# Tile-by-tile pool waits, an early start of the local attention's q and k, and a full-matrix variance in a post-LN decoder

## The chip, the core and the metric

The kernel runs on one NeuronCore of one Trainium2 chip, in float32. Its engines work side by side, each on its own in-order stream: TensorE (PE, with its weight loads shown as PEld), VectorE (DVE), ScalarE (ACT), GpSimd (POOL), and SyncE (SP), which here only starts DMAs. Matmuls write PSUM; DVE and ACT read it; POOL works on SBUF. The metric is the time of one execution on the device in microseconds, lower is better. Before the change it is 2500.81 us, the median of three runs (2500.76 to 2501.01).

## What is computed

Eight sequences of 256 tokens with 128 features pass three sublayers, each followed by a LayerNorm without gain and bias. Cut to what matters:

```python
# x: [8, 256, 128], ctx: [8, 256, 128]
x = layernorm(x + ssm(x))            # LN, conv over 4 tokens, SiLU, selective scan with 16 states, gate
x = layernorm(x + xattn(x, ctx))     # LN of x and of ctx; 16 heads of 64; scores clipped to +-11
x = layernorm(x + ffn(x))            # six layers, below

def ffn(x):
    for d in range(6):
        t = shift_tokens(x)                        # second half of the features from the token before
        q, k, v = split(t @ Wqkv[d], 3)            # 16 heads of 64
        q, k = rotary(l2norm(q) * qs[d]), rotary(l2norm(k) * ks[d])
        x = x + local_attention(q, k, v) @ Wo[d]   # window 32, looks at its own and the previous window
        h = LN(shift_tokens(x)) @ W1[d] + b1[d]
        x = x + (h_a * gelu(h_g)) @ W2[d] + b2[d]
    return x
```

## The kernel before

The features lie on the 128 partitions. Two sequences form a pair of 512 tokens (`TP`), and there are four pairs (`NPAIR`). Three stages follow one another.

**Stage 1** (to L494) runs the state-space sublayer pair by pair: `pre` (a LayerNorm, convolution, projections), `scan` (16 states by 2 halves) and `post` (the closing LayerNorm). Generators of the next and the last pair are advanced step by step inside `scan`. The first pair of stage 2's projections (`project(0)`) runs beside the last scan.

**Stage 2** (L497 to L573) is the cross attention. For each pair it runs 16 items (batch, pair of heads): `weights` (L504) makes scores on PE (L514), clips them on DVE (L520), takes Exp on ACT and adds two halves on POOL (L523); two items later `values` (L526) multiplies by v and sums on PE (L533, L539), takes the reciprocal by Ln and Exp on ACT, and divides on DVE (L546). Beside it `project(p + 1)` (L184) makes q, k and v of the next pair: two LayerNorms and twelve projections, one step per item. For the last pair (p = 3) nothing runs beside. Then come the output projection y2 (L566), the residual r (L570) and the pair's LayerNorm. q, k and v of even pairs lie in a pool on the right side of SBUF (`s2a`), those of odd pairs in the stage's own pool (`s2`), which also holds the items' tiles. `early2.close()` (L573) frees `s2w` (the weights) and `s2a`.

**Stage 3** (L576 to L951) is the six-layer transformer. Its pools `s3c`, `s3w` and `s3` are opened after stage 2's are closed. It clears the padded key tile `kz` (POOL, L589) and three padded value tiles `vz` (DVE, L592), loads rotary tables, mask and the weights of layer 0, and then works through 48 units `seq` of (layer, batch). A list `slots` (L902) gives the hand-made order of the steps in one round `run(n)` (L925): the attention of unit n, with q, k and v of units n + 1 and n + 2 in between, and the feed-forward of the last finished pair as a generator in the "ff" slots. The steps named below are `shift` (copies the shifted tokens, L653 to L655), `query_key` (one projection of 128 tokens to 1024 columns, L663; Square L675 on ACT; two multiplications with the rotary table, L682 and L683, and a sum of squares, L687, on DVE; two additions, L686, on POOL), `root` (a max on DVE, L695; Ln and Exp on ACT), `normalise` (POOL, L706), `turn` (transposes, L713), `value`, `scores` (L760) and `turn_weights` (L791). The rounds begin at n = −2, so that the first two rounds only fill the pipeline. PE's order in stage 3 is exactly the program's (`manual_schedule`, L941); the order on the other engines, and that of stages 1 and 2, is chosen by a scheduler. Four LayerNorms (L950) and the transposing store (L157) end the kernel.

**LayerNorm** (`layernorm_steps`, L101) works on [128 features, 512 tokens]. The mean comes from a matmul with a full matrix of 1/128 (L104), which leaves the mean on every partition; DVE subtracts (L108), ACT squares (L110). The variance comes from four matmuls with one column (L115), so it lies with tokens on partitions as 128x4; ACT takes Ln and Exp of that (L89), and four matmuls with the identity (L128) spread it over all partitions again; DVE multiplies (L135 or L137). `yield`s split it into steps for whoever advances it; with `fine` they lie before other steps than without.

**Pools.** A pool of tiles that is opened where an older one lay waits, at the first use of any of its tiles, for all the older pool's work (`reuse_waits="pool"`, the default). PSUM has one pool for stages 2 and 3 (`ps`, L498) and another for stage 1 (`ps1`), with two buffers for each of the tags "big", "s" and "o".

Of the kernel before, what the change touches and what calls it, by code (L numbers as in the profile page):

```python
# [49 lines left out]
def decoder_kernel(ctx: ExitStack, tc: tile.TileContext, a: dict, out: bass.AP):  # L50
# [8 lines left out]
    def psum(name):  # L59
        return tc.tile_pool(name=name, bufs=2, space=bass.MemoryType.PSUM)  # L60
# [40 lines left out]
    def layernorm_steps(x, dst, g=None, b=None, view=lambda t: t, fine=False):  # L101

        mu = ps_s("ln_mu")
        T.matmul(mu, lhsT=mean_w, rhs=x, start=True, stop=True)  # L104
        if fine:
            yield
        xc = lnp.tile([P, TP], FP, name="ln_xc")
        V.tensor_tensor(xc, x, mu, ALU.subtract)  # L108
        sq = lnp.tile([P, TP], FP, name="ln_sq")
        A.activation(sq, xc, AF.Square)  # L110
        if not fine:
            yield
        var = ps_s("ln_var")
        for j in range(4):
            T.matmul(  # L115
                var[:, j : j + 1], lhsT=sq[:, j * P : (j + 1) * P], rhs=mean_w[:, 0:1],
                start=True, stop=True,
            )
        if fine:
            yield  # L120
        rs = lnp.tile([P, 4], FP, name="ln_rs")
        inv_root(rs, var[:, 0:4], eps_t)
        if not fine:
            yield

        bc = ps_s("ln_bc")
        for j in range(4):
            T.matmul(  # L128
                bc[:, j * P : (j + 1) * P], lhsT=rs[:, j : j + 1].to_broadcast([P, P]), rhs=ident,
                start=True, stop=True,  # L130
            )
        if fine:
            yield
        if g is None:
            V.tensor_tensor(dst, xc, bc, ALU.mult)  # L135
        else:
            V.scalar_tensor_tensor(dst, view(xc), g, view(bc), ALU.mult, ALU.mult)  # L137
            V.tensor_scalar(dst, dst, b, None, ALU.add)
# [33 lines left out]
    pools2 = [early2.enter_context(tc.tile_pool(name="s2a", bufs=1, side="right"))]  # L172
# [325 lines left out]
    banks.append(ctx.enter_context(psum("ps")))  # L498
    with tc.tile_pool(name="s2", bufs=2) as sp:
# [51 lines left out]
        for p in range(NPAIR):  # L551
            cur, nxt = nxt, {}
            ahead = project(p + 1, nxt) if p + 1 < NPAIR else iter(())
# [15 lines left out]
            r = sp.tile([P, TP], FP, name="r2")  # L569
            V.scalar_tensor_tensor(r, y_ps, col("bo"), x1[p], ALU.add, ALU.add)  # L570
            x2[p] = new_x(p)
            layernorm(r, x2[p])
# [3 lines left out]
    with ExitStack() as st:  # L576
        cp = st.enter_context(tc.tile_pool(name="s3c", bufs=1))
        wp = st.enter_context(tc.tile_pool(name="s3w", bufs=2))
        sp = st.enter_context(tc.tile_pool(name="s3", bufs=2))

        rot = cp.tile([P, 4, 2, HD], FP, name="rot")
        nc.sync.dma_start(out=rot, in_=a["c_rot"])
        mask = cp.tile([P, NW, 2 * W], FP, name="mask")
        nc.sync.dma_start(out=mask, in_=a["c_mask"])


        kzs = [cp.tile([P, NHB, 2, W + S], FP, name=f"kz{i}") for i in range(1)]
        for t in kzs:
            G.memset(t, 0.0)  # L589
        vzs = [cp.tile([P, 4, 4, 2, HD], FP, name=f"vz{i}") for i in range(3)]  # L590
        for t in vzs:
            V.memset(t, 0.0)  # L592

        x3 = [new_x(p) for p in range(NPAIR)]
        wts, thirds, tabs = {}, {}, {}

        def load_third(d, c):

            w = wp.tile([P, INNER], FP, name="wqkv", bufs=4)
            nc.sync.dma_start(out=w, in_=a["L0_ffn_Wqkv"][d][:, c * INNER : (c + 1) * INNER])  # L600
            thirds[d, c] = w

        def load_table3(d):
            sc = wp.tile([P, 2, HD], FP, name="sc", bufs=1)
            for i, src in enumerate((a["L0_ffn_q_scale"], a["L0_ffn_k_scale"])):
                nc.sync.dma_start(out=sc[:, i, :], in_=src[d : d + 1, :].to_broadcast([P, HD]))

            tab = wp.tile([P, 4, 2, HD], FP, name="tab")
            for i in range(2):
                V.tensor_tensor(  # L610
                    tab[:, 2 * i], rot[:, 2 * i],
                    sc[:, i].unsqueeze(1).to_broadcast([P, 2, HD]), ALU.mult,
                )
                for u in range(2):
                    o, f = slice(u * 32, u * 32 + 32), slice(32 - u * 32, 64 - u * 32)
                    V.tensor_tensor(
                        tab[:, 2 * i + 1, :, f], rot[:, 2 * i + 1, :, o],
                        sc[:, i, f].unsqueeze(1).to_broadcast([P, 2, 32]), ALU.mult,
                    )
            tabs[d] = tab  # L620

        def load(d):
            wo = wp.tile([P, NHB, D], FP, name="wo3")
            nc.sync.dma_start(out=wo, in_=a["L0_ffn_Wo"][d].rearrange("(k p) e -> p k e", p=P))
            w1 = wp.tile([P, 2 * DFF], FP, name="w1")
            nc.sync.dma_start(out=w1, in_=a["L0_ffn_W1"][d])
            w2 = wp.tile([P, 3, D], FP, name="w2")
            nc.sync.dma_start(
                out=w2[:, 0:2, :], in_=a["L0_ffn_W2"][d][0:256].rearrange("(k p) e -> p k e", p=P)
            )  # L630
            nc.sync.dma_start(out=w2[: DFF - 256, 2, :], in_=a["L0_ffn_W2"][d][256:DFF])
            wts[d] = wo, w1, w2

        def batch(xs, b):
            return xs[b // 2][:, (b % 2) * S : (b % 2 + 1) * S]

        seq = [(d, b) for d in range(DEPTH) for b in range(B)]
        todo = [(wh, g) for wh in range(2) for g in range(2)]

        got = [{} for _ in seq]  # L640

        def shift(n):

            d, b = seq[n]
            if d + 1 < DEPTH:
                if b == 3:
                    load(d + 1)
                    load_table3(d + 1)
                if b == 6:
                    load_third(d + 1, 0)  # L650
            x = batch(x2 if d == 0 else x3, b)
            xs = sp.tile([P, S], FP, name="xs", bufs=3)
            G.memset(xs[HD:, 0:1], 0.0)  # L653
            A.copy(xs[:HD, :], x[:HD, :])
            A.copy(xs[HD:, 1:], x[HD:, : S - 1])  # L655
            got[n]["xs"] = xs
            got[n]["ss"] = sp.tile([P, 4, H], FP, name="ss", bufs=3)
            got[n]["rn"] = sp.tile([P, 4, H], FP, name="rn", bufs=3)

        def proj(n, c, tb, name):  # L660
            pr = ps_big(name)
            for i in range(2):
                T.matmul(  # L663
                    pr[:, i * 512 : (i + 1) * 512], lhsT=got[n]["xs"][:, tb * P : (tb + 1) * P],
                    rhs=thirds[seq[n][0], c][:, i * 512 : (i + 1) * 512], start=True, stop=True,
                )
            return pr

        def query_key(n, c, tb):

            d, b = seq[n]
            pr = proj(n, c, tb, "qk_ps")
            p3 = pr.rearrange("p (h d) -> p h d", h=H)
            sq = sp.tile([P, H, HD], FP, name="sq", bufs=1)
            A.activation(sq, p3, AF.Square)  # L675
            t = sp.tile([P, H, HD], FP, name="qk", bufs=4)
            rb = sp.tile([P, H, HD], FP, name="rb", bufs=1)
            cs, sn = (
                tabs[d][:, 2 * c + k, tb, :].unsqueeze(1).to_broadcast([P, H, HD])
                for k in range(2)  # L680
            )
            V.tensor_tensor(t, p3, cs, ALU.mult)  # L682
            V.tensor_tensor(rb, p3, sn, ALU.mult)  # L683
            for u in range(2):
                o, f = slice(u * 32, u * 32 + 32), slice(32 - u * 32, 64 - u * 32)
                G.tensor_tensor(t[:, :, o], t[:, :, o], rb[:, :, f], ALU.add)  # L686
            V.tensor_reduce(got[n]["ss"][:, 2 * c + tb, :], sq, AX.X, ALU.add)  # L687
            got[n][c, tb] = t
            if tb == 1 and b == B - 1 and d + 1 < DEPTH:
                load_third(d + 1, c + 1)  # L690

        def root(n, c, tb):

            ss, rn = (got[n][x][:, 2 * c + tb, :] for x in ("ss", "rn"))
            V.tensor_scalar(ss, ss, 1e-24, None, ALU.max)  # L695
            inv_root(rn, ss)

        def value(n, tb):
            t = sp.tile([P, INNER], FP, name="v3", bufs=4)
            A.copy(t, proj(n, 2, tb, "v_ps"))  # L700
            got[n]["v", tb] = t

        def normalise(n, c, tb):
            t = got[n][c, tb]
# [111 lines left out]
        def turn_output(n, t):  # L816
            wh, g = todo[t]
            if g == 0:
                got[n]["oT", wh] = sp.tile([P, NHB, P], FP, name="oT3")
# [218 lines left out]
```

## Time and profile before

The profiled execution took 2499.94 us; its span, from the first to the last instruction recorded, is 2498.2 us. Stretches of it, by the first instruction of each:

| stretch | from, us | first instruction |
|---|---|---|
| stage 1 | 0 | |
| stage 2, pair 0 | 383.1 | scores L514 |
| pair 3, alone | about 624 | scores L514 |
| y2 of pair 3 | 677.46 to 683.74 | L566 |
| stage 3, first projection | 693.32 | L663 |
| rounds with attention (n = 0) | 737.73 | L791 |
| closing LayerNorms and store | 2462.55 | L104 |

In the profile, a group of instructions is written as line, engine, operation, names of what is written and read, shapes, and their number; then busy time and mean duration, and how long the engine stood idle before them and on what. A timeline row begins with its start and duration in us. "PEclk" is the clock that TensorE was granted, in tenths of full speed; elsewhere it is given as a fraction.

The share of busy time by engine is PE 92%, DVE 72%, ACT 59%, POOL 57%. The chain of work that ended last, followed back from the end, lies 43% on PE, 32% on DVE, 14% on ACT and 4% on POOL.

### The profile page before, as it was taken

What the parts mean: (1) busy time and instruction counts of PE and PEld (TensorE: products, weight loads), DVE (VectorE), ACT (ScalarE), POOL (GpSimd) and SP (SyncE); (2) the same over time, 40 slices, a digit from 0 to 9 for tenths busy, and PEclk for the clock granted to TensorE, in tenths of its full rate; (3) what the DMA queues carried; (4) which work ended last, traced back from release to release, by engine and by line L of the source; (5) the groups of instructions that cost most, each with busy time, mean ns of one, the idle gap of its engine ahead of it and who ended that gap; (6) DMA issues with size and microseconds to landing.
All of it is one profiled execution on the core that took longest, in us unless ns stands there. A gap on an engine that the chain in (4) does not pass through costs nothing.

```text
span 2498.2 us, 54483 instructions
## 1 busy us (share of the span) xinstructions
PE 2310.4 (92%) x21378; PEld 1456.9 (58%) x21378; DVE 1795.9 (72%) x2661; ACT 1462.7 (59%) x2400; POOL 1432.0 (57%) x1180
## 2 busy tenths in 40 slices
PE   7688789999879999999999999999999999999996
PEld 3233235554446666666666666666666666666664
DVE  4788874444477777777777778777777877777762
ACT  4444444444446666666666666666666666666652
POOL 3889882222367665665656656666655666656630
PEclk9898899999979999999999999999999999999997
DMA  4444430000032223222222223222232223222220
GB/s 125 96 112 108 100 76 5 5 1 1 1 111 65 56 64 72 68 62 59 71 65 69 60 56 82 65 66 56 64 73 62 68 54 75 56 56 56 58 56 17
DMA packets 437963, 154.62 MB, mean 62 GB/s; under 512 B 401295, under 2 KB 417549, under 8 KB 437581
## 3 DMA queue, kind: packets, MB, share of 16 engines
q1 hardware_dynamic: 437708, 151.14, 25.0%
q8 instruction: 171, 2.80, 0.5%
q14 instruction: 84, 0.68, 0.1%
HBM read 55.33 MB, written 1.31 MB: 23 GB/s over the span
## 4 chain that ended last, share of the span: by engine, by line
PE 43%; DVE 32%; ACT 14%; POOL 4%; issue 3%; DMA 2%; SPq 1%; ACTq 0%; DVEq 0%; POOLq 0%
DVE qk L682 6%; DVE rb L683 6%; PE qk_ps L663 6%; DVE ss L687 6%; PE f_ps L869 3%; PE o_ps L803 3%; DVE on L810 3%; PE qkT_ps L713 3%; PE f_ps L894 2%; ACT sq L675 2%; PE s_ps L514 2%; PE o_ps L533 2%; DVE m L423 2%; POOL mc L425 2%; PE y_ps L835 2%
## 5 line engine op out<-in xcount | busy, mean ns | idle before, releaser
L686 POOL TENSOR_TENSOR qk<-qk,rb 128x512 f32<-128x512 f32 x384 | 481.0, 1274 | 434.4 <-DVE rb L683 288.3
L706 POOL TENSOR_TENSOR qk<-qk,rn 128x1024 f32<-128x1024 f32 x192 | 369.3, 1924 | 31.9 <-ACT rn L89 29.4
L682 DVE TENSOR_TENSOR qk<-qk_ps,tab 128x1024 f32<-128x1024 f32 x192 | 234.9, 1223 | 207.3 <-ACT sq L675 207.3
L663 PE MATMUL qk_ps<-wqkv,xs 128*128 128x512 f32 x768 | 373.7, 610 | 7.8 <-issue 3.1
L774 POOL TENSOR_TENSOR pw<-pw,mx 128x512 f32<-128x512 f32 x192 | 200.5, 1044 | 160.4 <-DVE mx L773 106.7
L725 ACT COPY kz<-qkT_ps 64x1024 f32<-64x1024 f32 x192 | 193.4, 1007 | 119.5 <-PE qkT_ps L713 117.5
L803 PE MATMUL o_ps<-vz,pT 128*32 128x128 f32 x6144 | 207.5, 276 | 29.7 <-ACT pT L795 27.1
L687 DVE TENSOR_REDUCE ss<-sq 128x16 f32<-128x1024 f32 x192 | 232.0, 1208 | 4.0 <-ACT sq L675 4.0
L683 DVE TENSOR_TENSOR rb<-qk_ps,tab 128x1024 f32<-128x1024 f32 x192 | 233.1, 1214 | 1.5 <-POOL qk L686 1.5
L783 DVE TENSOR_REDUCE mx<-pw 128x8 f32<-128x512 f32 x192 | 130.7, 681 | 140.9 <-ACT pw L89 138.7
L720 ACT COPY qT<-qkT_ps 128x1024 f32<-128x1024 f32 x96 | 97.2, 1013 | 218.7 <-PE qkT_ps L713 218.2
L803 PEld LDWEIGHTS o_ps<-vz,pT 128*32 128x32 f32 x6144 | 156.0, 109 | 118.3 <-ACT pT L795 107.2
L675 ACT ACTIVATE sq<-qk_ps 128x1024 f32<-128x1024 f32 x192 | 195.5, 1018 | 44.2 <-PE qk_ps L663 39.4
L713 PE MATMUL qkT_ps<-ident,qk 128*128 128x128 f32 x1536 | 211.1, 281 | 6.8 <-POOL qk L706 4.1
L523 POOL TENSOR_TENSOR ws<-w 128x512 f32<-128x512 f32 x64 | 81.4, 1272 | 216.5 <-ACT w L89 138.7
L760 PE MATMUL s_ps<-kz,qT 128*32 128x128 f32 x6144 | 203.1, 273 | 0.0
L406 PE MATMUL y<-mc,ident 128*128 128x512 f32 x256 | 153.3, 707 | 49.0 <-POOL mc L425 47.8
L663 PEld LDWEIGHTS qk_ps<-wqkv,xs 128*128 128x128 f32 x768 | 134.6, 195 | 106.3 <-issue 103.0
L713 PEld LDWEIGHTS qkT_ps<-ident,qk 128*128 128x128 f32 x1536 | 166.0, 142 | 47.8 <-issue 41.3
L835 PE MATMUL y_ps<-oT,wo 128*128 128x128 f32 x1536 | 187.7, 275 | 1.5 <-DVE ln_xc L108 0.9
L663 PE MATMUL v_ps<-wqkv,xs 128*128 128x512 f32 x384 | 181.7, 595 | 0.0
L835 PEld LDWEIGHTS y_ps<-oT,wo 128*128 128x128 f32 x1536 | 179.2, 192 | 2.2 <-DVE ln_xc L108 1.1
(155 smaller groups left out, 4358.4 us busy)
## 6 DMA issues: line engine op xcount, KB each, us to landing
vz<-v SPq DMA_DIRECT2D x1152, 64.0 KB, 2.2
rows<-bc_dram SPq DMA_DIRECT2D x128, 256.0 KB, 4.1
vz<-v SPq DMA_DIRECT2D x576, 32.0 KB, 2.4
wqkv<-in_L_ffn_Wqkv SPq DMA_DIRECT2D x18, 512.0 KB, 4.4
wo<-in_L_ffn_Wo SPq DMA_DIRECT2D x6, 512.0 KB, 7.1
w<-in_L_ffn_W SPq DMA_DIRECT2D x6, 341.0 KB, 3.3
t_in<-in_x SPq DMA_DIRECT2D x4, 256.0 KB, 3.8
wkv<-in_L_xattn_Wkv SPq DMA_DIRECT2D x1, 1024.0 KB, 8.1
```

Of the source, the lines that this page charges most:

```text
L663: T.matmul(pr[:, i * 512 : (i + 1) * 512], lhsT=got[n]["xs"][:, tb * P : (tb + 1) * P], rhs=thirds[seq[n][0], c][:, i * 512 : (i + 1) * 51 ...
L675: A.activation(sq, p3, AF.Square)
L682: V.tensor_tensor(t, p3, cs, ALU.mult)
L683: V.tensor_tensor(rb, p3, sn, ALU.mult)
L686: G.tensor_tensor(t[:, :, o], t[:, :, o], rb[:, :, f], ALU.add)
L687: V.tensor_reduce(got[n]["ss"][:, 2 * c + tb, :], sq, AX.X, ALU.add)
L706: G.tensor_tensor(t, t, r, ALU.mult)
L713: T.transpose(t_ps[:, hb * P : (hb + 1) * P], t[:, 2 * hb : 2 * hb + 2, :].rearrange("p h d -> p (h d)"), ident,)
L760: T.matmul(s_ps[i * W : (i + 1) * W, j * P : (j + 1) * P], lhsT=qT[:, 4 * g + i, j * W : (j + 1) * W], rhs=kz[:, 4 * g + i, :, k0 : k0 + 2 ...
L774: G.tensor_tensor(pw, pw, mx[:, 0].unsqueeze(3).to_broadcast(shape), ALU.subtract)
L803: T.matmul(o_ps[i * W : (i + 1) * W, j * P : (j + 1) * P], lhsT=pT[:, j, i * W : (i + 1) * W], rhs=vz[:, j, i].rearrange("p e d -> p (e d) ...
L835: T.matmul(y_ps[:, :P], lhsT=wts[d][0][:, hb, :], rhs=got[n]["oT", wh][:, hb, :], start=(hb == 0), stop=(hb == NHB - 1),)
```

## The change

It has three parts.

1. *Waits.* `psum` takes a mode, and the pools `ps`, `s2` and those of stage 3 are opened with `reuse_waits="tile"`: a tile waits only for the tiles that lay where it lies, not for a whole pool. Stage 1's pools stay as they were.
2. *Variance.* `layernorm_steps` has a form `wide=True`, the default: one matmul with the full 1/128 matrix gives the variance on every partition, Ln and Exp run on 128x512 in place of the squares, and DVE multiplies from there. The one-column matmuls, the 128x4 Ln and Exp, the spreading matmuls and one PSUM tile go. Only `feed_forward` asks for the old form. Of 48 LayerNorms, 24 become wide: eight in stage 1 proper, eight in `project`, four at the ends of stage 2's pairs and four at the kernel's end.
3. *Early start.* Stage 3's helper functions are moved ahead of stage 2, with their tiles in dictionaries (`pools3`, `fixed3`). For p = 3 a new generator `begin()` takes the place of `project`: it opens two pools of stage 3 on the right side, where `s2a` is closed first, loads the rotary table, layer 0's weights and scales, and makes q and k of batch 0, one step per item. `run` leaves out what is in `done`. The rounds start at n = −1. The last pair's LayerNorm is not run at once but put in `ff`, so that the "ff" slots of round −1 advance it. `r` is a tile of the pool of x. All memsets of `kz` and `vz` are on POOL, and the mask is loaded after `begin()`.

```diff
-    def psum(name):
-        return tc.tile_pool(name=name, bufs=2, space=bass.MemoryType.PSUM)
+    def psum(name, waits="pool"):
+        return tc.tile_pool(name=name, bufs=2, space=bass.MemoryType.PSUM, reuse_waits=waits)
...
-    def layernorm_steps(x, dst, g=None, b=None, view=lambda t: t, fine=False):
+    def layernorm_steps(x, dst, g=None, b=None, view=lambda t: t, fine=False, wide=True):
...
+        if wide:
+
+            var = ps_s("ln_var")
+            T.matmul(var, lhsT=mean_w, rhs=sq, start=True, stop=True)
+            if fine:
+                yield
+            inv_root(sq, var, eps_t)
+            if not fine:
+                yield
+            bc = sq
+        else:
...
+    right2 = ctx.enter_context(ExitStack())
+    pools2 = [right2.enter_context(tc.tile_pool(name="s2a", bufs=1, side="right"))]
...
+    def run(n):
...
+            elif 0 <= n + k < len(seq) and (f, n + k, *args) not in done:
+                f(n + k, *args)
...
+    def begin():
+
+        for name in ("w", "a"):
+            pools3[name] = ctx.enter_context(
+                tc.tile_pool(name=f"s3{name}", bufs=2, side="right", reuse_waits="tile")
+            )
+        fixed3["rot"] = pools3["w"].tile([P, 4, 2, HD], FP, name="rot", bufs=1)
+        nc.sync.dma_start(out=fixed3["rot"], in_=a["c_rot"])
+        for c in range(3):
+            load_third(0, c)
+        load_table3(0)
+        load(0)
+        yield
+        steps = [(shift, 0)]
+        for c in range(2):
+            for tb in range(2):
+                steps += [(query_key, 0, c, tb), (root, 0, c, tb), (normalise, 0, c, tb)]
+        for f, *args in steps:
+            f(*args)
+            done.add((f, *args))
+            yield
...
+    banks.append(ctx.enter_context(psum("ps", "tile")))
+    with tc.tile_pool(name="s2", bufs=2, reuse_waits="tile") as sp:
...
-            ahead = project(p + 1, nxt) if p + 1 < NPAIR else iter(())
+            if p == NPAIR - 1:
+                right2.close()
+            ahead = project(p + 1, nxt) if p + 1 < NPAIR else begin()
...
-            r = sp.tile([P, TP], FP, name="r2")
+            r = new_x(p)
             V.scalar_tensor_tensor(r, y_ps, col("bo"), x1[p], ALU.add, ALU.add)
             x2[p] = new_x(p)
-            layernorm(r, x2[p])
+            if p < NPAIR - 1:
+                layernorm(r, x2[p])
+            else:
+                ff = layernorm_steps(r, x2[p])
...
+        for t in fixed3["kzs"] + fixed3["vzs"]:
             G.memset(t, 0.0)
-        vzs = [cp.tile([P, 4, 4, 2, HD], FP, name=f"vz{i}") for i in range(3)]
-        for t in vzs:
-            V.memset(t, 0.0)
...
-            shift(0)
-            for n in range(-2, len(seq)):
+            shift(1)
+            for n in range(-1, len(seq)):
                 run(n)
```

## The prediction

> **What bounds the kernel now.** I read the page's shares first, then a table of windows (one row for each stage), then the timeline at the seams. From the page:
>
> ```profile
> PE 2310.4 (92%) x21378; PEld 1456.9 (58%) x21378; DVE 1795.9 (72%) x2661; ACT 1462.7 (59%) x2400; POOL 1432.0 (57%) x1180
> ...
> PEclk9898899999979999999999999999999999999997
> ```
>
> TensorE (PE) is the bound overall, but an average hides the seams, and this change touches mostly seams. The windows (stretch, length, busy PE, PEld, DVE, ACT, POOL, granted clock, DMA share, GB/s):
>
> ```profile
> 543.00:624.00 81.00, 80.30 (x442) 41.71 (x441) 36.31 (x45) 39.34 (x66) 20.35 (x16) 1.00 0.00 1
> 624.00:677.00 53.00, 47.15 (x343) 26.60 (x343) 26.87 (x34) 26.81 (x49) 20.34 (x16) 1.00 0.00 1
> 677.00:707.00 30.00, 21.06 (x50) 9.27 (x46) 15.23 (x20) 6.57 (x15) 8.33 (x8) 0.75 0.53 162
> 707.00:738.00 31.00, 23.29 (x123) 12.56 (x124) 25.65 (x30) 14.31 (x23) 21.40 (x18) 0.75 0.16 37
> 738.00:2462.00 1724.00, 1655.03 (x18778) 1147.31 (x18777) 1325.62 (x1989) 1121.17 (x1840) 1025.46 (x817) 0.99 0.27 63
> 2462.00:2498.00 36.00, 21.37 (x90) 14.89 (x88) 6.86 (x10) 6.74 (x16) 0.00 (x0) 0.76 0.10 30
> ```
>
> See four things. Pairs 0 to 2 of stage 2 (row 543) are full on PE; pair 3 (row 624), with no projection beside it, leaves PE 53 − 47.15 = 5.85 us idle and DVE half idle. The start of stage 3 (677 to 738) and the tail have idle PE **and** a clock of 0.75. Layers 0 to 5 (738 to 2462) are full. The seam in the timeline:
>
> ```profile
> 683.78 0.75 DVE L570 SCALAR_TENSOR_TENSOR r<-y_ps,cols,x 128x512 f32<-128x512 f32 x1 [4.91 <-PE y_ps L566]
> ...
> 686.58 3.94 POOL L589 MEMSET kz<- 128x4608 f32 x1 [9.98 <-DVE ln_xc L108]
> ...
> 687.15 1.05 PE L115 MATMUL ln_var<-mean_w,ln_sq 128*128 128x1 f32 x8 [1.44 <-ACT ln_sq L110]
> ...
> 689.21 2.07 PE L128 MATMUL ln_bc<-ident,ln_rs 128*128 128x128 f32 x8 [1.01 <-ACT ln_rs L89]
> ...
> 693.32 6.31 PE L663 MATMUL qk_ps<-wqkv,xs 128*128 128x512 f32 x8 [2.03 <-DMA wqkv<-in_L_ffn_Wqkv]
> ```
>
> The first memset of stage 3 starts only when the last LayerNorm's subtract is done (the pool wait), the weights are fetched only then, and the first projection waits for them.
>
> **The steady loop.** Laid side by side, the two programs have the same order on all five engines and the same producers behind each wait from batch 1 of layer 0 to the last feed-forward; its LayerNorm keeps the old form. I cost 738 to 2462 at **0**.
>
> **Wide variance, stages 1 and 2.** Each wide LayerNorm drops eight ln_var and eight ln_bc passes on PE (1.05 us, and 1.16 us at full clock in stage 2, 2.07 at half) and two small ACT operations (0.26, 0.20); it adds one matmul like ln_mu (1.02 to 1.13 us) and two ACT passes over 128x512, nearest row the Square of L110, 0.63 each. PE gains about 1.1 us, ACT loses 2 × 0.63 − 0.46 = 0.8.
> - First LayerNorm, at half clock: var + bc 1.86 + 2.07 becomes about 2.1 + 0.8: **−1**.
> - Edge of stages 1 and 2: from Square's end (378.99) to the first scores (383.10) is 4.1 us. The first scores now follow the variance matmul and wait for its Ln alone (PSUM buffer), about 1.9 us: **−2**.
> - Stage 1 between: its pitch is POOL's (mc 1.27 + dw 1.04 per state and half, sum near the measured 2.22); PE and DVE have slack. ACT's order moves: two gate SiLUs of pairs 2 and 3 are split, two more table loads each (1.28 us). ACT is 45% busy, so the cover is there, but it feeds POOL. **0**, ends −3 and +5.
> - Stage 2, pairs 0 to 2: eight LayerNorms × 1.16 = 9.3 at most; where a LayerNorm runs beside an item the pace is 3.4 to 3.5 us, and pair 3 shows the latency floor, 2.98 per item, so two items give back 1 us at most, and less when the next item is full. Ends −3 and −9, **−6**.
>
> **q and k of batch 0 beside pair 3.** In come: DMAs (rot, three thirds, scales, wo, w1, w2) on SP, four projections on PE (4 × 4 passes × 0.43 = 6.9 us), on ACT four Squares and eight roots (5.8) and the copies for the shift (0.8), on DVE four × (1.22 + 1.21 + 1.21 + 0.2) = 15.3 and a table of 1.4, on POOL four × (2 × 1.27 + 1.90) = 17.8. PE's part less its idle 5.85 gives the low end, **+1**. But DVE runs in order: an item is clip 1.22, Exp 1.06, Ln and Exp 0.77, divide 0.42, then the next clip; a 1.2 us instruction of q/k that starts in a gap of 2.98 − 1.22 − 0.42 = 1.34 delays the divide or clip queued behind it by about half its length. 12 × 0.7 = 8.6; all of it in series gives +18. I take **+9**. The loads wait until pair 2's last scores have read the space below them, about 19 us before PE needs them, against 5.9 from issue to use now; were they late, DVE's table would hold the clips behind it.
>
> Here a rule speaks against the change. "SBUF — State Buffer", section "Who interferes with whom", in the Trainium skill: GpSimd and DVE share a port pair, a tensor_scalar in its two-port mode locks it for the whole instruction and the other waits. POOL rises to 38 of some 62 us in this stretch, and clip is a tensor_scalar. The rows (min/median/max ns, first the clips of pair 3, then the small max of the roots over the run):
>
> ```profile
> L520 DVE TENSOR_SCALAR w<-s_ps x16: 1214/1215/1225, 628.7 to 672.9; 128x1024 f32<-128x1024 f32 x16
> L695 DVE TENSOR_SCALAR ss<-ss x192: 118/183/1248, 702.5 to 2401.5; 128x16 f32<-128x16 f32 x192
> ```
>
> By the rule for every tensor_scalar: 16 clips × 0.6 chance × half of a 1.4 us POOL instruction = +6.7. By the row: the clip, which reads PSUM, never grows beside POOL's additions, while the SBUF-only max does, to 1.25: at most 4 × 1.07 = +4, inside the +18 end. I take the row.
>
> **From y2's end to the first turned weights.** Before: 683.74 to 737.73, 54.0 us. After, x2[3]'s LayerNorm lies in run(−1)'s feed-forward slots, and only this remains on PE: four turns 4 × 1.10, three projections of batch 1 and two of values, 5 × 1.72, three score tiles × 1.06, LayerNorm 2.2: 18.4 us. POOL: kz 3.94 and, moved from DVE, three vz 5.3, then three chunks × 4.44: 22.6. kz still waits for the last y2 matmul, since it lies over wo2; POOL queues the vz memsets before batch 1's sums, and those gate the second chunk's rb on DVE. Hence 21.5 by hand at full clock.
>
> "TensorE: Matmul & The Clock Gate" of the Trainium skill, "The HAM clock gate": half clock follows an idle window of some 3.4 us, and an equally long busy one restores it. After the change PE should have no idle gap above 2 us there, so by the rule 21.5 stands, a gain of 32.5. The trace says otherwise, with PE's largest gap in this window 1.6 us:
>
> ```profile
> 707.00:715.00 8.00, 6.15 (x13) 3.25 (x14) 7.96 (x9) 2.25 (x4) 5.43 (x5) 0.50 0.01 2
> ```
>
> Over 707 to 738 the clock is 0.75, so I take PE's 18.4 / 0.75 = 24.5, say **25**: −29; ends 21.5 (−32.5) and 32 (−22). Both parts: −29 + 9 = **−20**, ends −31 and −4.
>
> **Tail.** Four LayerNorms follow one another:
>
> ```profile
> 2464.15 0.68 DVE L108 TENSOR_TENSOR ln_xc<-x,ln_mu 128x512 f32<-128x512 f32 x1
> ...
> 2465.54 1.05 PE L115 MATMUL ln_var<-mean_w,ln_sq 128*128 128x1 f32 x8 [1.97 <-ACT ln_sq L110]
> ...
> 2467.19 2.08 PE L128 MATMUL ln_bc<-ident,ln_rs 128*128 128x128 f32 x8 [0.59 <-ACT ln_rs L89]
> ...
> 2470.67 0.69 DVE L108 TENSOR_TENSOR ln_xc<-x,ln_mu 128x512 f32<-128x512 f32 x1 [0.68 <-PE ln_mu L104]
> ```
>
> The next mean stands behind this pair's ln_bc: pitch 6.68. After, it stands behind ln_var: mean 1.1, subtract 0.68, Square 0.63, var 1.1, gaps 0.2: 3.7 at full clock, 5.9 at half; at the tail's 0.76 about 4.4. Three pitches × 2.3 and 1.4 in the last: **−8.5**, ends −4 and −10.5.
>
> **Sum.** −1 − 2 + 0 − 6 − 20 − 8.5 = −37.5 from the profiled execution's 2499.94 (span 2498.2): 2462.4. The median of the runs is 0.9 above it, so about **2463**.
>
> **Rivals.**
> - *The cover is free* (0.18): pair 3 absorbs q and k in its idle halves, +1 for +9, and the seam runs at full clock: −31; sum −48, **2452**. For it: DVE half idle, clock 1.00 there. Against: DVE's order.
> - *Displaced, not hidden* (0.22): chain and q/k serialise on DVE, +18, and run(−1) is paced by POOL's memsets, 32 us: −4; with the rest −21.5, **2479**. For it: POOL's 22.6 and DVE's contention rows.
> - *Slower* (0.04): the weights for begin() arrive so late that DVE's table multiplication, in order before the clips, stops pair 3. Nothing overlaps then. The price decides from a stall of 38 us, against 19 us of lead and 5.9 us of loading: say 45, **2508**.
> - *It does not do what it says* (0.03): space below stage 3's tiles still belongs to pair 3, so everything starts where it did; only tail and edges remain, −11.5, 2489. Against: in the built program the memsets wait for y2's last matmul and the loads for pair 2's last scores, not for the pool.
>
> The forecast has 0.53, own range 2455 to 2471. A measurement here tells about 0.2% (5 us) from no change; faster 0.94, same 0.02, slower 0.04. Range 2446 to 2482.
>
> **What would show it.** Right: first turned weights about 25 us after y2's last matmul; pair 3 about 62 us long instead of 53; tail pitch near 4.4; from the first turned weights to the last feed-forward within 2 us of 1725. Wrong: a pair 3 above 70, a DVE wait on the table's DMA, a clock of 0.5 in the seam, or stage 1 longer than 388.

## The result and the profile after

The changed kernel takes 2469.85 us, the median of four runs (2468.66 to 2475.45), against 2500.78 before (2498.28 to 2501.01). The ratio is 0.9883, with a 95% interval of 0.9866 to 0.9900: some 30 us, or 1.2%, faster. The span of the profiled execution is 2468.0 us, against 2498.2.

The shares of the engines on the page of the changed kernel, with the granted clock of its 40 slices, say almost nothing of it:

```profile
PE 2271.8 (92%) x21042; PEld 1405.4 (57%) x21042; DVE 1785.2 (72%) x2658; ACT 1485.8 (60%) x2404; POOL 1439.4 (58%) x1183
...
PEclk8898899999999999999999999999999999999998
```

What tells is a list of lengths by stage, taken from the starts and ends of PE's instructions in the two traces: the first scores of stage 2, the first y2 matmul of each pair, the end of the last y2, the first turned weights of stage 3 and the first mean of the four closing LayerNorms.

| stretch, us | before | after | difference |
|---|---|---|---|
| stage 1, to the first scores | 383.1 | 400.3 | **+17.2** |
| pair 0, to its y2 | 72.0 | 69.5 | −2.5 |
| pair 1 | 81.8 | 77.8 | −4.0 |
| pair 2 | 81.8 | 77.8 | −4.0 |
| pair 3, to the end of y2 | 65.0 | 72.1 | +7.1 |
| end of y2 to first turned weights | 54.0 | 21.4 | **−32.6** |
| to the closing LayerNorms | 1724.8 | 1722.7 | −2.2 |
| tail | 35.6 | 26.5 | −9.1 |

The sum is −30.2. Stage 1 went the wrong way by 17 us. The three pairs gave more than forecast (−10.6 together, against −6), and the rest went about as forecast. The windows view (stretch, length, busy PE, PEld, DVE, ACT, POOL, clock, DMA share, GB/s) of the changed kernel, for pair 3, the seam behind it and the tail:

```profile
625.40:697.40 72.00, 66.31 (x375) 32.90 (x373) 44.42 (x63) 37.39 (x70) 37.54 (x28) 1.00 0.11 33
697.40:718.90 21.50, 17.19 (x122) 9.26 (x121) 13.15 (x17) 13.03 (x18) 16.92 (x12) 1.00 0.26 47
2441.50:2468.00 26.50, 12.96 (x33) 4.91 (x31) 6.60 (x10) 9.91 (x16) 0.00 (x0) 0.83 0.13 40
```

In pair 3 DVE is now busy 44.42 of 72 us, where it was 26.87 of 53, and the seam runs at full clock, where the seam before ran at 0.75.

Where stage 1 lost its time is seen at the boundary where pair 2's opening work meets the scan of pair 1. First the kernel before, in the timeline (start, duration, engine, line, operation, tiles, idle time before it and what ended it). `ab` is a decay factor that the scan needs, `conv` the convolution, `xm` its SiLU, `mc` POOL's product of the scan's output and C, one for each of the 128 scans:

```profile
156.44 0.69 ACT L89 ACTIVATE ab<-dt,aa 128x512 f32<-128x512 f32 x1 [1.58 <-DVE m L423]
158.25 0.69 ACT L89 ACTIVATE ab<-dt,aa 128x512 f32<-128x512 f32 x1 [1.12 <-DVE m L423]
...
158.96 1.28 ACT L327 ACT_TABLE_LOAD   x1
158.97 3.60 PE L319 MATMUL conv<-xn,w_tap 128*128 128x512 f32 x8
160.26 0.69 ACT L327 ACTIVATE xm<-conv,cols 128x512 f32<-128x512 f32 x1
162.60 0.69 ACT L327 ACTIVATE xm<-conv,cols 128x512 f32<-128x512 f32 x1 [1.66 <-PE conv L319]
...
170.21 1.26 POOL L425 TENSOR_TENSOR mc<-m,rows 128x512 f32<-128x512 f32 x1 [4.67 <-issue]
```

The same place in the changed kernel:

```profile
154.04 1.28 ACT L334 ACT_TABLE_LOAD   x1
...
160.23 7.86 PE L326 MATMUL conv<-xn,w_tap 128*128 128x512 f32 x16
...
164.69 0.69 ACT L334 ACTIVATE xm<-conv,cols 128x512 f32<-128x512 f32 x1 [9.37 <-PE conv L326]
168.13 0.69 ACT L334 ACTIVATE xm<-conv,cols 128x512 f32<-128x512 f32 x1 [2.75 <-PE conv L326]
168.83 1.28 ACT L93 ACT_TABLE_LOAD   x1
170.13 1.30 ACT L89 ACTIVATE ab<-dt,aa 128x512 f32<-128x512 f32 x2
170.85 2.42 DVE L430 TENSOR_TENSOR_SCAN m<-dw,ab 128x256 f32<-128x256 f32 x4 [8.04 <-ACT ab L89]
...
172.25 1.27 POOL L432 TENSOR_TENSOR mc<-m,rows 128x512 f32<-128x512 f32 x1 [12.90 <-PE d_ps L352]
```

Before, ACT makes four `ab` between the LayerNorm's Exp and the SiLU's table load (the last two are shown), and when it comes to the SiLU, the first half of the convolution is done. After, the table is loaded right behind Exp, and ACT stands 9.37 us before the SiLU of a convolution that PE has not begun. Every `ab` of the running scan is queued behind it. DVE waits 8.04 us for one, and POOL, which paces stage 1, stands 12.90 us instead of 4.67. (The waits view names PE's d_ps as POOL's releaser. That matmul ends about when POOL goes on; in the rows the chain is `ab`, scan, `mc`.) The boundary of pair 3 has the same stall. Two more executions with this stage 1, in runs below, have their first scores at 400.7 and 400.2 us, so the loss is no accident of one execution.

### The profile page after: what moved, and what is told of

It is laid out like the page before. It is cut to its first block, busy times and chain, and to the rows that moved or that the text cites. A ratio compares the mean times of both kernels' runs of the same rounds, so it can differ in the third digit from the quotient of the medians.

```text
span 2468.0 us, 53789 instructions
## 1 busy us (share of the span) xinstructions
PE 2271.8 (92%) x21042; PEld 1405.4 (57%) x21042; DVE 1785.2 (72%) x2658; ACT 1485.8 (60%) x2404; POOL 1439.4 (58%) x1183
## 4 chain that ended last, share of the span: by engine, by line
PE 37%; DVE 31%; ACT 15%; POOL 3%; issue 2%; DMA 1%; SPq 1%; ACTq 0%; POOLq 0%; DVEq 0%
DVE qk L594 6%; DVE ss L599 6%; DVE rb L595 6%; PE qk_ps L575 5%; PE f_ps L781 3%; PE o_ps L715 3%; ACT sq L587 3%; DVE on L722 3%; PE qkT_ps L625 3%; PE f_ps L806 3%; DVE mx L695 2%; PE s_ps L672 2%; PE v_ps L575 2%; PE s_ps L887 2%; ACT kz L637 2%
## 5 line engine op out<-in xcount | busy, mean ns | idle before, releaser
L575 PE MATMUL qk_ps<-wqkv,xs 128*128 128x512 f32 x768 | 364.5, 597 | 1.3 <-ACT qT L632 1.1
L430 DVE TENSOR_TENSOR_SCAN m<-dw,ab 128x256 f32<-128x256 f32 x256 | 160.7, 670 | 47.9 <-POOL mc L432 27.9
L432 POOL TENSOR_TENSOR mc<-m,rows 128x512 f32<-128x512 f32 x128 | 162.6, 1272 | 48.1 <-PE d_ps L352 24.1
```

Source lines behind the costliest of these rows:

```text
L575: T.matmul(pr[:, i * 512 : (i + 1) * 512], lhsT=got[n]["xs"][:, tb * P : (tb + 1) * P], rhs=thirds[seq[n][0], c][:, i * 512 : (i + 1) * 51 ...
```

## Experiments

The theory after this reading was that not the wide form's work but its place costs stage 1 its 20 us (17.2 in the table, and some 3 us that the wide form should have gained at its beginning and end). In `fine` mode the old LayerNorm yields three times and the wide one twice. A generator that yields once less does its later work one step of the scan earlier, and the scheduler then puts the convolution and its SiLU ahead of the `ab`s. The first rival is the wide form's own work (0.8 us more on ACT each time); the second, that stage 1 suffers from something else in the change.

**The old variance in stage 1 alone.** The ten LayerNorms of stage 1 get `wide=False`, with the old yields put back in that form.

```diff
-            yield from layernorm_steps(x, xn, col("ssm_g"), col("ssm_b"), two, p > 0)
+            yield from layernorm_steps(x, xn, col("ssm_g"), col("ssm_b"), two, p > 0, False)
...
-            yield from layernorm_steps(r, x1[p], fine=True)
+            yield from layernorm_steps(r, x1[p], fine=True, wide=False)
```

> The changed kernel, with the old variance (one-column matmuls, 128x4 Ln and Exp, spreading matmuls, with the old steps) in the ten LayerNorms that run in stage 1; the other 14 stay wide. Theory: stage 1 became 17 us longer (first scores of stage 2 at 400.3 instead of 383.1) through the wide LayerNorms there, so it returns to about 383 and the two long stalls of POOL (12.9 and 11.2 us) to about 4.7; the time falls from 2469.9 by 16 to 18 us, to 2452 to 2454. Rival: the longer stage 1 comes from the other parts (loads, pools, the hoisted code); then the first scores stay near 400 and the time near 2470.

Measured: 2454.92 us (ratio to the kernel before 0.9816, 0.9802 to 0.9831); first scores at 385.6. POOL's longest stall on `mc` is 5.0 us again. The order of instructions in stage 1 is that of the kernel before on PE, DVE, ACT and POOL; the 2.5 us between the first scores are no more than single executions of one order scatter (below). The LayerNorms of stage 1 are the cause, and the loads, pools and hoisted functions are not.

**One step more.** All LayerNorms stay wide.

```diff
             inv_root(sq, var, eps_t)
-            if not fine:
-                yield
+            yield
             bc = sq
```

> The changed kernel, with one yield more: in the fine steps of a wide LayerNorm, one after Ln and Exp, so that it has as many steps as the old one. All 24 stay wide. Theory 'order': the wide form has one step less, so the convolution and its SiLU table load come one step earlier on PE and ACT, ahead of decay factors (ab) that the scan needs; with the step back ACT has its ab before the table load again, the first scores come at 379 to 383 and the time falls by 18 to 21 us, to 2449 to 2452. Rival 'work': it is the wide form's own work, 0.8 us more on ACT per LayerNorm, that starves the scan; then the first scores stay within 4 us of 400 and the time above 2465.

Measured: 2452.21 us (0.9808, 0.9791 to 0.9824); first scores at 382.2. The wide form's work is all there, and the first scores come where they came before (383.1): 'work' falls, 'order' holds. The timeline of this kernel at the boundary shows three `ab` ahead of the table load (the first of them at 149.97), and SiLU waiting 2.94 instead of 9.37 us:

```profile
153.11 0.69 ACT L89 ACTIVATE ab<-dt,aa 128x512 f32<-128x512 f32 x1 [2.44 <-DVE m L429]
154.94 0.69 ACT L89 ACTIVATE ab<-dt,aa 128x512 f32<-128x512 f32 x1 [1.14 <-DVE m L429]
...
155.65 1.28 ACT L333 ACT_TABLE_LOAD   x1
...
159.87 0.69 ACT L333 ACTIVATE xm<-conv,cols 128x512 f32<-128x512 f32 x1 [2.94 <-PE conv L325]
...
168.33 1.26 POOL L431 TENSOR_TENSOR mc<-m,rows 128x512 f32<-128x512 f32 x1 [4.88 <-PE bc_ps L338]
```

**The step in the closing LayerNorms only, or in the opening ones only.** Both give one `ab` ahead of the table load at the boundaries of pairs 2 and 3. They differ at the boundary of pair 1.

> The changed kernel with the extra step only in the closing LayerNorms of stage 1. On ACT one decay factor (ab) then stands between the second LayerNorm's Exp and the SiLU table load at the boundaries of pairs 2 and 3, where the changed kernel has none, the version with the step everywhere three, and before four; the boundary of pair 1 is as in the changed kernel (none). Theory 'order': the stall shrinks with each ab that stands ahead; first scores between 386 and 394, time 2456 to 2464. Rival: only the number of wide LayerNorms counts; first scores at 400, time near 2470.

> The changed kernel with the extra step only in the LayerNorms that open pairs 1 to 3 of stage 1. Boundaries of pairs 2 and 3 are as with the step in the closing LayerNorms (one ab ahead of the table load); at the boundary of pair 1 two ab come ahead instead of none. Theory 'order': faster than the run with the closing step by what pair 1 lost, about 4 us (its scan of pair 0 fell from 1.8 us ahead of the kernel before to 2.1 us behind it): first scores 382 to 390, time 2452 to 2460. Rival: both runs are the same within 1.5 us, and the boundary of pair 1 costs nothing.

Measured: 2459.04 us (first scores 389.8) and 2456.24 us (388.5). Both lie between none and three, as 'order' says. Between the two, the first scores differ by 1.3 us only, which would be the rival's "within 1.5"; but stage 1 does not begin alike in all executions (the first `mc` comes between 39.3 and 42.8 us, in one order of instructions too). From the first `mc` to the 25th, which leaves the beginning out, the runs take 71.2 and 67.6 us (71.2 in the changed kernel, 67.2 before): the boundary of pair 1 costs its 4 us.

The same measure over the boundary of pair 2 (from the 41st `mc`) and of pair 3 (from the 73rd) sets the runs in order. It is taken over 16 `mc` and over 32; undisturbed, they would take 16 × 2.22 = 35.5 us and 71.0 us.

| `ab` ahead of the SiLU's table load | pair 2, 16 `mc` | pair 3, 16 `mc` | pair 2, 32 `mc` | pair 3, 32 `mc` |
|---|---|---|---|---|
| none (after) | 53.6 | 52.4 | 90.7 | 90.1 |
| one (closing step only; opening step only) | 48.7; 48.2 | 48.1; 48.3 | 85.8; 85.3 | 86.3; 86.0 |
| three (one step more) | 46.1 | 46.0 | 83.9 | 84.7 |
| four (before; the old variance in stage 1) | 45.2; 45.3 | 45.3; 45.2 | 81.9; 82.9 | 83.6; 83.5 |
| five or four, SiLUs split (two steps more) | 38.0 | 38.4 | 80.1 | 81.1 |
| seven, SiLUs split (three, two and one steps more) | 38.7 | 39.1 | 78.8 | 80.3 |
| nine, SiLUs split (three steps more) | 39.4 | 39.3 | 81.4 | 83.9 |

From none to four the two measures agree. In the last three rows the SiLUs of the gate come only behind the 57th and the 89th `mc` (in the run with two steps their table load starts at 192.4 us, 8.5 us behind the 57th), so the measure over 16 leaves their stall out and flatters these runs; the one over 32 has it in. A second execution of the two-step order, in the last run below, took 39.9, 38.4, 80.3 and 78.4 us, so the last three rows are not apart.

**Two steps more, and three.** These runs were a surprise.

> The changed kernel with two extra steps in every fine wide LayerNorm. Five ab come ahead of the table load at the boundaries of pairs 2 and 3, but the scheduler then splits the two SiLUs there and loads two more tables (1.28 us each) at each. Theory 'order': no stall is left to gain, and the extra loads cost ACT 5 us in all, part of it hidden: first scores 381 to 387, time 2450 to 2457. Rival: each step is worth as much as the first; first scores below 378.

> The changed kernel with three extra steps in the opening LayerNorms of stage 1's pairs, two in the closing ones and one in those of the first projection: seven ab ahead of the table load at the boundaries of pairs 2 and 3 instead of five with two steps everywhere, and the SiLUs still split. Theory 'order': what is left to gain is small, because PE's convolution no longer is what ACT waits for; stage 1 within 3 us of the 377.4 of the two-step version, time 2441 to 2448. Rival: each two ab ahead are still worth 3 us or more; first scores below 374.5.

> The changed kernel with three extra steps in every fine wide LayerNorm: nine ab ahead of the table load at the boundaries of pairs 2 and 3; the next pair's decay steps and the projections of stage 2 are pushed later, towards the end of the scan. Theory 'order': a delay too far makes the next pair's first inputs late; first scores 376 to 386, not better than the two-step version (377.4). Rival: later is always better; first scores below 374.5 and time below 2440.

Measured: 2443.32 us (0.9765, 0.9749 to 0.9781), first scores 377.4; 2440.86 us (0.9764, 0.9740 to 0.9788), 371.5; and 2449.23 us, 380.4. The first expectation failed: two more table loads at each boundary were to cost, and the runs are faster. Over 32 `mc` two steps gain 3.6 to 3.8 us at a boundary on one step more, and 1.8 and 2.5 us on the kernel before. (The rival's mark, below 378, was met, but not what it says: the first step was worth 18 us of stage 1, the second 4.8.) The rows of ACT with two steps more:

```profile
162.01 1.28 ACT L335 ACT_TABLE_LOAD   x1
...
165.68 0.69 ACT L335 ACTIVATE xm<-conv,cols 128x512 f32<-128x512 f32 x1 [2.38 <-PE conv L327]
166.38 1.28 ACT L89 ACT_TABLE_LOAD   x1
...
167.68 1.30 ACT L89 ACTIVATE ab<-dt,aa 128x512 f32<-128x512 f32 x2
...
169.00 1.28 ACT L335 ACT_TABLE_LOAD   x1
...
170.83 0.69 ACT L335 ACTIVATE xm<-conv,cols 128x512 f32<-128x512 f32 x1 [0.55 <-PE conv L327]
171.53 1.28 ACT L93 ACT_TABLE_LOAD   x1
```

Two `ab` stand between the two SiLUs, so the scan goes on while PE makes the second half of the convolution. At pair 3's boundary four `ab` stand ahead, as in the kernel before, and the split is what differs; that it makes the gain is a reading of these rows, since no run changed the split alone.

The second expectation failed too: first scores at 371.5 are 5.9 us ahead of 377.4, where at most 3 were expected, and meet the rival's mark. But the second execution of the two-step order had its first scores at 370.7, on another chip, the one on which 371.5 was measured. Single executions of one order in stage 1 thus lie up to 6.6 us apart, and whether 3, 2, 1 steps are better than 2 everywhere is not settled; the ratios agree. Three steps everywhere did not improve on two, as expected.

**Without the early q and k.** Nothing runs beside pair 3; the loads still start as early as their space allows, and the rounds begin at −2.

```diff
-            if p == NPAIR - 1:
-                right2.close()
-            ahead = project(p + 1, nxt) if p + 1 < NPAIR else begin()
+            ahead = project(p + 1, nxt) if p + 1 < NPAIR else iter(())
...
+    right2.close()
+    next(begin())
     early2.close()
...
-            shift(1)
-            for n in range(-1, len(seq)):
+            shift(0)
+            for n in range(-2, len(seq)):
```

> The changed kernel without the early q and k: nothing runs beside pair 3, the loads of begin() come as early as their space allows, and the rounds start at -2 again; tile waits, wide variance and the last pair's LayerNorm in the rounds stay. Theory: pair 3 (72.0 us from its start to the end of y2, 64.9 before) falls to about 63, and the stretch from y2's end to the first turned weights (21.4 us, 54.0 before) grows to 42 to 48; together 12 to 18 us slower, 2482 to 2488. Rival 'displaced': early q and k only move work; both stretches together change by less than 4 us, and the time stays at 2467 to 2474.

Measured: 2482.02 us, 12.2 slower than the changed kernel. Pair 3 falls to 65.0 us (−7.1), the stretch behind y2 grows to 42.2 (+20.8). So early q and k take 20.8 us off the seam and add 7.1 to pair 3, 13.6 net in the two profiles. The other 12 of the seam's 32.6 us are there without them; the earlier loads and the LayerNorm put into the rounds are what is left to explain them, and no run took these two apart. Windows of this run behind y2:

```profile
688.90:700.00 11.10, 6.98 (x15) 2.79 (x16) 5.85 (x7) 3.13 (x5) 10.52 (x7) 1.00 0.00 0
700.00:715.00 15.00, 8.11 (x18) 3.53 (x16) 10.28 (x12) 5.48 (x11) 11.63 (x9) 0.77 0.02 3
715.00:731.00 16.00, 12.18 (x104) 7.08 (x105) 12.51 (x16) 9.52 (x15) 12.30 (x11) 1.00 0.34 62
```

PE is busy 8.11 of 15 us in the middle window, and the clock falls to 0.77 there; with q and k done early PE has no such hole, and the clock stays at 1.00.

**Pool waits again.** All pools of stages 2 and 3 back to `reuse_waits="pool"`, early q and k kept.

> The changed kernel with all pools waiting for whole pools again; early q and k, the deferred LayerNorm and the wide variance stay. Theory: tile waits are worth little by themselves, because the tiles that stage 3 starts with lie over the last things read anyway; the first scores come about 1 us later and the stretch after y2 stays at 21 to 23 us: 2470 to 2473. Rival: the tile waits carry the shorter seam; then the stretch after y2 grows by 5 us or more and the time is above 2475.

Measured: 2471.65 us, 1.8 slower; first scores 400.2, so not later; pair 3 73.7 us (72.1 with tile waits), 21.5 us behind y2. With early q and k in place the tile waits are worth some 2 us, in pair 3 and not in the seam; without early q and k they were not tried.

**The old variance everywhere.** `wide=False` as the default, with the old yields.

> The changed kernel with the old variance in all LayerNorms: what is left is the waits, the early q and k and the deferred LayerNorm. Theory: stage 1 at 383 to 386; pairs 0 to 2 as long as before (72.0, 81.8, 81.8 us; with the wide form 69.5, 77.8, 77.8); pair 3 at 72 to 74; 22 to 24 us from y2's end to the first turned weights; tail 33 to 36 us instead of 26.5: 2474 to 2480. Rival: pairs 0 to 2 became shorter by the tile waits, or the tail's gain is only the clock; then the pairs stay below 79 us and the time below 2470.

Measured: 2477.13 us. Stage 1 385.1, pairs 71.4, 81.8 and 81.8, pair 3 73.0, seam 20.8, tail 35.6. The gains in pairs 0 to 2 and in the tail are the wide variance's alone; the seam, a little below the 22 to 24 expected, owes nothing to it.

**vz cleared on VectorE, as before.** On the version with two steps more.

```diff
-        for t in fixed3["kzs"] + fixed3["vzs"]:
+        for t in fixed3["kzs"]:
             G.memset(t, 0.0)
+        for t in fixed3["vzs"]:
+            V.memset(t, 0.0)
```

> The version with two extra steps everywhere, and the three vz memsets on VectorE as in the kernel before. Theory: the stretch from y2's end to the first turned weights (21.5 us) is held by POOL's memsets of 9.2 us, behind which the sums of batch 1's first q and k stand; with 3.9 us there it falls to 18 to 20.5 us: 1 to 3 us faster than 2443.3. Rival: VectorE's chain of that stretch pays as much as POOL saves; it stays at 21 to 23 us.

Both theories failed: the stretch behind y2 grew to 29.1 us, and the time to 2449.86. (Of the profiled executions, against two steps more: stage 1 −6.6 us, in the same order; seam +7.6; tail +2.6, in the same order too.) The timeline of this run shows what neither had counted:

```profile
668.58 1.13 PE L104 MATMUL ln_mu<-x,mean_w 128*128 128x512 f32 x2
668.90 1.76 DVE L966 MEMSET vz<- 128x2048 f32 x1 [0.38 <-DVE x L945]
671.04 1.76 DVE L966 MEMSET vz<- 128x2048 f32 x1 [0.38 <-issue]
673.18 1.76 DVE L966 MEMSET vz<- 128x2048 f32 x1 [0.38 <-issue]
674.86 0.63 DVE L108 TENSOR_TENSOR ln_xc<-x,ln_mu 128x512 f32<-128x512 f32 x1
675.53 0.63 ACT L110 ACTIVATE ln_sq<-ln_xc 128x512 f32<-128x512 f32 x1 [5.81 <-DVE ln_xc L108]
676.21 2.07 PE L116 MATMUL ln_var<-ln_sq,mean_w 128*128 128x512 f32 x2 [6.50 <-ACT ln_sq L110]
678.08 3.52 PE L575 MATMUL v_ps<-wqkv,xs 128*128 128x512 f32 x4
```

The deferred LayerNorm stands in PE's fixed order. With the memsets ahead of its subtract on DVE, PE stands 6.50 us before ln_var, with all of batch 1's projections behind it, and the matmuls that follow run at half speed (values 3.52 us, 1.88 in the changed kernel; the granted clock is 0.66 from 676 to 684 us). Where vz is cleared is part of the deferral, not a detail.

## Why the prediction was right, and where it was wrong

The direction, the time (2463 forecast, 2469.85 measured) and the seam as the main source were right. That the time came within 7 us is in part luck: stage 1 was 20 us worse than forecast, and the other steps together 13 us better. One of the prediction's own signs of being wrong came true, a stage 1 longer than 388 us (400.3). By its steps:

- **Steady loop, 0.** Measured −2.2; runs with the same order there lie between 1722.7 and 1725.5, so it is none.
- **First LayerNorm −1, edge −2.** −1.8 by the first `mc` (whose scatter is larger) and −1.2: from Square's end to the scores 2.9 us, since ln_var ran at half clock (2.07).
- **Stage 1 between, "0, ends −3 and +5".** This is the step that failed: +20.2 (the 17.2 of the table and the 1.8 and 1.2 gained at its two ends). The three boundaries hold 19.5 of it: +3.9 from the first `mc` to the 25th, +8.4 from the 41st to the 57th, +7.2 from the 73rd to the 89th. The prediction saw that ACT's order had moved, but priced the split gate SiLUs as 1.28 us for each table load, with ACT's 45% as cover. There it was right: from the 49th `mc` to the 65th, where the split SiLUs of pair 2's gate stand, the changed kernel is 1.0 us quicker. The cost lay at another instruction, the SiLU of the convolution (POOL 12.90 us idle for 4.67), and it was not work but a place: in an in-order queue, what waits for PE was put ahead of what feeds DVE and POOL.
- **Pairs 0 to 2, −6.** −10.6, beyond the end of −9. A LayerNorm gives back its whole PE time: in pairs 1 and 2 PE is busy 77.3 us where it was 81.1, 3.8 of the 4.05 us, or 1.27 for each of three LayerNorms where 1.16 was called the most. The items' latency floor held nothing back.
- **Pair 3, +9.** +7.1, near the number but by another sum. The +9 was a dozen delays of 0.7 us behind DVE, with all but 1 us of PE's own 6.9 us of projections fitted into its 5.85 us of idle time. The window of pair 3 before, from its start to the end of y2, beside the one of 72.00 us above:

```profile
618.77:683.74 64.97, 59.12 (x371) 31.60 (x369) 27.30 (x35) 28.62 (x52) 20.34 (x16) 1.00 0.00 1
```

  PE is busy 7.2 us longer (66.31 for 59.12) and stands idle as long as before (5.7 for 5.85). None of the idle time was used: PE's new work came on top in full. The waits have changed their cause. Before, PE waited 5.1 us in all for the division on DVE (oT); after, it waits 3.4 us for DVE's rb, four times (two of them below), and 1.7 us for POOL's sums. So the delays behind DVE are there, but four and not twelve.

```profile
646.20 1.13 PE L887 MATMUL s_ps<-qT,kT 64*128 64x256 f32 x8 [1.32 <-DVE rb L595]
...
657.07 1.13 PE L887 MATMUL s_ps<-qT,kT 64*128 64x256 f32 x8 [0.70 <-DVE rb L595]
```

  The row was rightly taken over the rule of "SBUF — State Buffer" applied to every tensor_scalar; the page itself has tensor_scalar contend only when its operands meet conditions, so the row does not speak against it. With POOL busy 37.54 of 72 us the clips of pair 3 did not grow (second row: not even the small max did). The multiplications of the rotary table on DVE, both inputs in SBUF, did grow: two of the four that ran beside a POOL sum took 0.94 and 1.29 us where those of their shape otherwise take 0.28 and 0.22, some 1.7 us in all (third row, one of their two shapes):

```profile
L893 DVE TENSOR_SCALAR w<-s_ps x16: 1209/1216/1225, 635.3 to 686.6; 128x1024 f32<-128x1024 f32 x16
...
L607 DVE TENSOR_SCALAR ss<-ss x4: 160/166/168, 648.6 to 681.2; 128x16 f32<-128x16 f32 x4
...
L528 DVE TENSOR_TENSOR tab<-rot,sc x8: 214/218/1291, 633.3 to 642.2; 128x64 f32<-128x64 f32 x8
```

- **Seam, 25 us.** 21.4. Here the row was wrongly taken over the rule of "TensorE: Matmul & The Clock Gate". The clock of 0.75 belonged to a stretch with holes of 3.05 and 3.26 us in PE; the changed stretch has none above 1.54, and the hand-made 21.5 at full clock was right. The rule gave the figure, but no gap in the seam before reached its 3.4 us either, and the clock fell there all the same; the last section has the rows. (PE's list had one score tile too many, two stand there; PE is busy 17.2 us.)
- **Tail, −8.5.** −9.1, with clock 0.83 and starts of the four means 4.0, 5.2 and 4.1 us apart (6.5, 6.5 and 6.8 before, so the 6.68 of the sum was a little high). In six other runs the tail took 23.9 us, with a clock of 0.89 to 0.96, PE busy 10.36 us in place of 12.96 (one step more). The gap of 2.6 us is the clock's, in one and the same order.

The rivals: the time alone does not choose, since 2469.85 lies between the forecast's 2463 and the 2479 of "displaced". By the stages, "displaced" (+18 and 32 us) and "does not do what it says" fall with 7.1 and 21.4 us and with the run without early q and k; "the cover is free" was right for the seam alone; "slower" did not come, since no load was late.

## What to carry to other kernels

Where generators are advanced step by step beside an in-order engine, a yield is part of the schedule: taking out work together with its step moves everything behind it earlier, and should be checked by what now stands ahead of what in the queue of each engine. A function-table load marks the danger here: the activation behind it waited for TensorE, and what another chain needs from ScalarE should be ahead of it. Two more loads to let work through between two such activations did no harm in these runs. Forecast seams from the work that remains in them at the clock of a filled stretch, not at the clock of the old one with its holes.

## What was not expected of the hardware

Two more table loads (2.6 us of ScalarE) at a boundary went with 3.6 to 3.8 us less over the 32 `mc` around it than one step more without them; the order of the `ab` differs too.

The granted clock in the seam was 1.00 with PE busy 17.2 of 21.5 us, and 0.50 in the kernel before with PE busy 6.15 of 8 us: nearly the same share. The trace of the kernel before shows more when its windows are cut where the clock changes, at steps of 3.41 us (columns as above):

```profile
698.64:702.05 3.41, 0.99 (x3) 0.16 (x1) 3.41 (x9) 1.02 (x1) 0.00 (x0) 1.00 0.85 242
702.05:705.46 3.41, 2.78 (x4) 1.18 (x4) 1.95 (x4) 0.43 (x2) 2.65 (x3) 0.50 0.55 175
705.46:708.88 3.42, 2.61 (x10) 1.57 (x8) 3.38 (x5) 0.36 (x3) 3.42 (x3) 0.50 0.02 5
708.88:712.29 3.41, 1.81 (x4) 0.84 (x3) 3.41 (x4) 1.89 (x3) 2.80 (x2) 0.50 0.00 0
712.29:715.71 3.42, 3.42 (x5) 1.18 (x4) 3.42 (x5) 0.30 (x1) 1.46 (x2) 0.50 0.00 0
715.71:719.12 3.41, 1.22 (x3) 0.19 (x1) 3.41 (x5) 2.02 (x4) 1.91 (x2) 1.00 0.05 12
```

Full clock was lost behind a step with PE busy 0.99 us of 3.41. Three steps with PE busy 2.78, 2.61 and 1.81 us did not bring it back; one in which PE was busy throughout did. Here it took less work to keep full clock than to regain it: the changed seam has a stretch of 3.4 us with PE busy 1.86 us (714.4 to 717.8) and stays at 1.00. In all thirteen traces every return from 0.50 to 1.00 stands behind a step with PE busy 83% or more; not every such step is followed by one, and the rule was not tried further.

Stage 1 of one and the same order took 377.4 and 370.7 us in two executions, on two chips. The fastest kernel here by its median, with three, two and one steps more, takes 2440.86 us, 0.9764 of the time before; two steps everywhere cannot be told from it (0.9765).
